# A two-layer decoder in one kernel: softmax probabilities turned by VectorE in squares of 32 and moved to their rows through DRAM

## The chip, the cores and the metric

The kernel runs on one core of a Trainium2 chip. A core has a matrix engine (TensorE), a vector engine (VectorE), a scalar engine (ScalarE), a general engine (GpSimd) and an engine that mainly issues transfers (SyncE, "SP" in the profile). Each has its own instruction stream; they meet through semaphores. The metric is the device time of one execution in microseconds (us): the median of the kernel before is 2106.39 us over three runs (2104.89 to 2107.31).

## What is computed

The input `x` is 16 sequences of 128 tokens with 512 features, all in 32-bit floats, and a context of 16 times 128 tokens with 128 features. Two decoder layers follow each other. In each, three sublayers are added to `x`, and each sum is normalized:

```
x = LN(x + attention(x));  x = LN(x + cross(x, ctx));  x = LN(x + ffn(x))
```

- Layer 0, attention: 16 heads of 32 features share 4 key and value heads. A mask of 1 on and below the diagonal is added to the scores, then softmax, values, an output projection with a bias.
- Layer 0, cross attention: 16 heads over the context, with key and query weights that the kernel first multiplies together ("folds").
- Layer 0, FFN: two ternary input weights, a gate, and a ternary output weight.
- Layer 1, attention: a linear attention with decay; it has no softmax.
- Layer 1, cross attention: 16 heads of 32 features, causal mask, scores divided by the root of 32, softmax, output projection.
- Layer 1, FFN: a shared expert, and eight experts of which each token uses two.

The change touches the first attention and the last cross attention. These have the same core, for each sequence and head:

```
p = softmax(q @ k.T * scale + mask)      # 128 queries x 128 keys
out = p @ v                              # then out @ wo.T over all heads
```

The scores come out with a query on each of the 128 partitions (rows of on-chip memory), since softmax sums along a row. TensorE sums over partitions, so for `p @ v` the keys have to be on the partitions: every `p` must be transposed, 16 matrices of 128x128 for each sequence.

## The kernel before

A block is one sequence (`P` = 128 tokens), of which there are `NB` = 16; a group is `GB` = 4 blocks, and there are `NG` = 4 groups. `x` stays on chip, one tile a block. PSUM, in which TensorE writes its results, has eight banks; `psum.share` (line 75) deals them out by tag: `mm` for projections and the transposes of `x`, `sc` for scores, `pt` for transposed probabilities and for the values' result. In both attentions it gives `mm` 2, `sc` 4, `pt` 2.

The sublayers run one after the other: the first attention at about 34 to 260 us of the profiled execution, the latent cross attention to 755, the ternary FFN to 1062, the linear attention to 1290, the last cross attention (the second one that the change touches; its first projections lie between 1290 and 1314) to 1522, routing and the shared expert to 1700, the experts to the end.

Both softmax attentions use one loop, `attend` (line 227). It is software pipelined over `n` from 0 to 17: `score(n)` issues the 16 small score matmuls of block `n` into four banks, one for each chunk of four heads. `value(n - 2)` multiplies the turned probabilities of the block two earlier with its values into a `pt` bank; ScalarE copies that to `oT` (line 246). Then come four steps, one for each chunk `c`:

- `Softmax.start`: VectorE adds the mask into a tile `t` (line 184) and takes the row maximum (line 186); ScalarE takes four exponentials with their row sums (line 191).
- `Softmax.finish`, for the chunk one earlier: VectorE takes the reciprocal of the sums (line 197) and GpSimd scales `p` (line 198).
- `Softmax.turn`, for chunk `c` of block `n - 1`: four TensorE transposes into a `pt` bank (line 203), and a VectorE copy to `pT` (line 205).
- at `c == 1` the output projection of block `n - 2`, `project_out` (line 144): four matmuls `po` (line 148), the residual add on VectorE (line 149), the statistics (line 110 on) and the normalization on GpSimd (line 121). At the other steps `share.deal()` issues a share of the next group's preparation.

The preparation (`prepare`) transposes four blocks of `x` on TensorE (lines 127 and 128), and projects queries, keys and values with 512-column matmuls (line 137, `chain`; tiles `pq`, `pk`, `pv`). In the first attention, preparation tasks of the later groups also hold the folding of the cross attention's weights (`fold`, line 274; its result `pg` in line 304). The weights to fold come as tiles `raw` of 1.7 MB each, two buffers, loaded by SP (line 391); a load waits for the fold two before it. After the last group, four of these folds and the rotation of the context (`dkv`, line 383) are what is left.

In the last cross attention each block's `x` is stored to a DRAM table `sums` as soon as it is normalized (line 987); the experts' results are added into that table later. Two tables in DRAM, `slots_x` (the tokens sorted by expert) and the tail of `sums`, must be zero before the experts start. The kernel writes these zeros (10 MB each) at the start of that cross attention's preparation (lines 897 to 899): GpSimd sets a tile `zero`, and two DMAs spread it.

A scheduler orders the instructions of each engine by the program and its own planned costs. SP issues nearly all transfers on one queue, in order: an issue that has to wait for a semaphore holds up all behind it.

The FFN between (`p3`, from line 672) runs over the four groups; its weights `w1`, `w2`, `w3` come in pieces of 352 KB through SP, and behind them the weights `wq4` of the linear attention. The latent cross attention turns its own probabilities otherwise: VectorE transposes within squares of 32 (line 590).

## Time and profile before

| | |
|---|---|
| median of three runs | 2106.39 us (2104.89 to 2107.31) |
| the profiled execution | 2109.23 us |
| its span on the core | 2107.5 us |
| busy: TensorE, weight loads | 2053.2 us (97%), 1148.5 us (54%) |
| busy: VectorE, ScalarE, GpSimd | 853.9 us (41%), 626.0 us (30%), 648.2 us (31%) |
| transposes of `p`, 128 x 4 on TensorE, copies on VectorE | 86.5 us of VectorE for the 128 copies (678 ns each) |
| scaling on GpSimd (three attentions) | 192 x 1048 ns = 201.1 us |
| exponentials of the masked attentions on ScalarE | 512 x 390 ns = 198.6 us |
| moved by DMA | 209.99 MB, 100 GB/s over the span |

The profiled execution's time is a little above the median, and its span is 1.7 us shorter than its time. Busy times are sums of instruction durations; those of TensorE overlap in the pipeline, so that the time a matmul adds is read from the distance of two starts, not from its duration. In lines that list instructions the tile written stands left of `<-`, the tiles read right of it, then shapes and the count. A clock of 1.00 is TensorE's full speed; the mean of this execution is 0.995. An entry such as "idle before, releaser" says how long an engine stood before the instructions of a group and what ended most of it.

### The profile page before, as it was taken

How to read it: one execution, taken by the hardware profiler on the slowest of the kernel's cores; microseconds unless marked ns; L12 is line 12 of the kernel's file. 1: busy time of each engine (PE TensorE's matmuls, PEld its weight loads, DVE VectorE, ACT ScalarE, POOL GpSimd, SP SyncE). 2: the span in 40 equal slices, each digit the busy share in tenths (PEclk: the TensorE clock that was granted, in tenths of full speed). 3: DMA queues.
4: the chain of work that ended last, by engine and by line, in shares of the span. 5: the costliest groups of instructions: out<-in, count | busy, mean ns of one | idle time of the engine just before them, and what ended most of it. 6: DMA issues, size and time to landing. Idle time of an engine off the chain costs nothing. (4 is left out here: it accounts for less than half of the span.)

```text
span 2107.5 us, 26857 instructions
## 1 busy us (share of the span) xinstructions
PE 2053.2 (97%) x10117; PEld 1148.5 (54%) x10117; DVE 853.9 (41%) x1728; ACT 626.0 (30%) x2167; POOL 648.2 (31%) x674
## 2 busy tenths in 40 slices
PE   8999999999999999999999999999899999999997
PEld 5555554445454458888555444555544455555552
DVE  4667733444554243222123313777731122222224
ACT  3655533323333222222211112766622200000002
POOL 5565521211122122223223113455603222222223
PEclk9999999999999999999999999999999999999999
DMA  6011320212220010001300008600004279999974
GB/s 230 1 35 45 112 79 24 62 43 74 60 66 6 1 54 2 1 1 39 115 1 1 1 6 258 232 21 21 27 25 147 93 244 284 303 294 293 289 229 166
DMA packets 105362, 209.99 MB, mean 100 GB/s; under 512 B 27280, under 2 KB 65552, under 8 KB 98576
## 3 DMA queue, kind: packets, MB, share of 16 engines
q1 hardware_dynamic: 90336, 101.40, 15.4%
q0 software_dynamic: 13792, 105.55, 15.2%
q8 instruction: 80, 1.31, 0.3%
q10 hardware_dynamic: 1104, 1.31, 0.2%
q14 instruction: 50, 0.41, 0.1%
HBM read 159.66 MB, written 48.57 MB: 99 GB/s over the span
## 5 line engine op out<-in xcount | busy, mean ns | idle before, releaser
L198 POOL TENSOR_TENSOR p<-p,rs 128x512 f32<-128x512 f32 x192 | 201.1, 1048 | 505.4 <-DVE rs L197 478.3
L613 PE MATMUL po<-mT,cc 128*128 128x512 f32 x512 | 236.0, 605 | 0.0
L191 ACT ACTIVATE p<-t,nmx 128x128 f32<-128x128 f32 x512 | 198.6, 390 | 34.5 <-POOL p L198 8.8
L613 PEld LDWEIGHTS po<-mT,cc 128*128 128x128 f32 x512 | 92.2, 189 | 107.2 <-issue 103.6
L191 ACT ACTIVATE p<-sc,nmx 128x128 f32<-128x128 f32 x256 | 90.2, 373 | 147.4 <-DVE nmx L186 142.1
L114 POOL TENSOR_SCALAR ve<-mv 128x1 f32<-128x1 f32 x80 | 18.1, 227 | 328.2 <-DVE mv L112 316.2
L559 PE MATMUL pq<-xT,wqr 128*128 128x512 f32 x256 | 117.5, 602 | 1.0 <-ACT xT L128 0.7
L1171 ACT ACTIVATE rsg<-rg 128x352 f32<-128x352 f32 x39 | 18.1, 464 | 336.0 <-PE rg L1166 336.0
L148 PE MATMUL po<-wo,oT 128*128 128x512 f32 x256 | 116.8, 599 | 0.4 <-ACT qkT L416 0.4
L1166 PE MATMUL rg<-ew,xsT 128*128 128x352 f32 x312 | 101.2, 466 | 14.5 <-DMA ew<-in_l1f_w_dram,which 12.7
L783 PE MATMUL pq<-xT,wq 128*128 128x512 f32 x256 | 110.9, 594 | 1.0 <-ACT xT L128 0.7
L1187 PE MATMUL ry<-ew,ractT 128*128 128x512 f32 (+1 forms) x234 | 106.9, 592 | 0.0
L121 POOL TENSOR_SCALAR x<-x,mv,rstd 128x512 f32<-128x512 f32 x48 | 100.6, 2097 | 4.5
L1166 PE MATMUL ru<-ew,xsT 128*128 128x352 f32 x312 | 98.7, 459 | 0.0
L191 ACT ACTIVATION_READ_ACCUMULATOR p<-t,nmx 128x1 f32 x512 | 96.4, 188 | 0.0
L706 POOL TENSOR_TENSOR hl<-ht,hh 128x512 fp32r<-128x512 f32 x44 | 60.5, 1375 | 114.8 <-ACT hh L704 114.8
L1137 POOL DMA_INDIRECT ew<-in_l1f_w_dram,which x39 | 38.1, 976 | 185.9 <-PE ry L1187 163.3
L1197 POOL DMA_INDIRECT sums<-ry,place x39 | 62.0, 1590 | 105.7 <-DMA sums<-ry,place 66.4
L205 DVE COPY pT<-pt 128x512 f32<-128x512 f32 x128 | 86.5, 678 | 18.1 <-PE pt L203 18.1
L203 PEld LDWEIGHTS pt<-ident,p 128*128 128x128 f32 x512 | 59.8, 141 | 53.8 <-issue 44.6
L1049 PE MATMUL pg<-xT,sw_gu 128*128 128x512 f32 x192 | 86.5, 593 | 0.0
L1173 DVE TENSOR_TENSOR ract<-rsg,ru 128x352 f32<-128x352 f32 x39 | 20.3, 521 | 158.5 <-issue 145.5
(231 smaller groups left out, 3715.4 us busy)
## 6 DMA issues: line engine op xcount, KB each, us to landing
piece<-in_l0f_w_dram SPq DMA_DIRECT2D x48, 352.0 KB
raw<-in_l0x_raw_dram SPq DMA_DIRECT2D x8, 1728.0 KB
slots_x<-zero SPq DMA_DIRECT2D x1, 10023.0 KB
sums<-zero SPq DMA_DIRECT2D x1, 9984.0 KB
xs<-slots_x SPq DMA_DIRECT2D x156, 64.0 KB
rep<-dkv SPq DMA_DIRECT2D x64, 64.0 KB
sums<-x SPq DMA_DIRECT2D x16, 256.0 KB
sum<-sums SPq DMA_DIRECT2D x16, 256.0 KB
```

Of the source, the lines that this page charges most:

```text
L121: engine.tensor_scalar(x[b], x[b], mean, rstd, ALU.subtract, ALU.mult)
L148: nc.tensor.matmul(po, lhsT=oT[:, c, :], rhs=wo[:, c, :], start=(c == 0), stop=(c == KC - 1))
L191: nc.scalar.activation(self.p[:, j, :], src[:, j, :], AF.Exp, bias=nmx[:, j : j + 1], accum_out=self.sm[:, j : j + 1])
L198: nc.gpsimd.tensor_tensor(self.p, self.p, spread(rs, P), ALU.mult)
L205: nc.vector.tensor_copy(self.pT, pt)
L559: nc.tensor.matmul(pq, lhsT=wqr[:, k, cols], rhs=xT[:, k, :], start=(k == 0), stop=(k == KC - 1))
L613: nc.tensor.matmul(self.po, lhsT=self.cc[:, 4 * par + j, :], rhs=mT[h], start=(par == 0 and j == 0), stop=(par == 1 and j == 3),)
L783: nc.tensor.matmul(pq, lhsT=wq4[k // 2][:, k % 2, c * P : (c + 1) * P], rhs=xT[:, k, :], start=(k == 0), stop=(k == KC - 1))
L1049: nc.tensor.matmul(dst, lhsT=sw_gu[:, k, at : at + P], rhs=xTs[g][:, k, :], start=(k == 0), stop=(k == KC - 1),)
L1166: nc.tensor.matmul(dst, lhsT=self.xT[:, k, :], rhs=gu[:, k, off : off + FE], start=(k == 0), stop=(k == KC - 1),)
L1187: nc.tensor.matmul(po, lhsT=self.actT[:mw, m_, :], rhs=dn[:mw, m_, :], start=(m_ == 0), stop=(m_ == 2))
L1197: nc.gpsimd.indirect_dma_start(out=sums, out_offset=bass.IndirectOffsetOnAxis(ap=place, axis=0), in_=y, in_offset=None, compute_op=ALU.add,)
```

## The change

The probabilities of the two attentions are no longer transposed by TensorE.

- `Softmax.start` adds the mask straight into the tile `p` (five buffers); the tile `t` is gone.
- A class `Turn` takes the place of `Softmax.turn`. `squares(c, p)` is one VectorE transpose for each chunk of four heads, which turns every 32x32 square in place and orders the result by key square. After each second chunk one SP store moves the pair (512 KB) to a DRAM tile `away` (two buffers). After the fourth, `back` reads it in four SP loads: load `k` brings the squares of keys 32`k` to 32`k`+31 to partitions 32`k` to 32`k`+31 of `pT`, a tile for all 16 heads with one buffer.
- In `attend`, `squares` of a chunk is called two chunk steps after its `start`; `value(n - 2)` and the copy to `oT` move from the head of the iteration to step 1, and the output projection to step 2.
- Both `value` functions read the new `pT`, in runs of 32 elements, and issue their matmuls in program order.
- In both attentions `psum.share` gives `mm` 3, `sc` 4, `pt` 1.
- The tables `slots_x` and `sums` and their clearing move to the FFN: issued in its second group (`g == 1`), in program order.

```diff
-    psum.share(mm=2, sc=4, pt=2)
+    psum.share(mm=3, sc=4, pt=1)
...
         def start(self):
+            if self.p is None:
+                self.p = self.pool.tile([P, 4, P], F32, tag="p", name="p", bufs=5)
             src = self.sc
             if self.mask is not None:
-                src = self.pool.tile([P, 4, P], F32, tag="t", name="t", bufs=3)
+                src = self.p
                 nc.vector.tensor_tensor(src, self.sc, bc(self.mask, 4), ALU.add)
...
-        def turn(self):
-            pt = bank("pt", [P, 4, P], "pt")
-            for j in range(4):
-                nc.tensor.transpose(pt[:, j, :], self.p[:, j, :], ident)
-            self.pT = self.pool.tile([P, 4, P], F32, tag="pT", name="pT", bufs=4)
-            nc.vector.tensor_copy(self.pT, pt)
+    class Turn:
...
+        def __init__(self, pool):
+            self.pool = pool
+            self.away = dram.tile([P, 4, 2, 8 * Q], F32, tag="away", name="away", bufs=2)
+
+        def squares(self, c, p):
+            if c % 2 == 0:
+                self.sq = self.pool.tile([P, 4, 8, Q], F32, tag="sq", name="sq", bufs=2)
+            at = slice(c % 2 * 4, c % 2 * 4 + 4)
+            nc.vector.transpose(
+                self.sq[:, :, at, :].rearrange("p k h q -> p h k q"), p.rearrange("p h (k a) -> p h k a", a=Q)
+            )
+            if c % 2:
+                nc.sync.dma_start(self.away[:, :, c // 2, :], self.sq.rearrange("p k h q -> p k (h q)"))
+            if c == 3:
+                self.back()
+
+        def back(self):
+            self.pT = self.pool.tile([P, 4, 16, Q], F32, tag="pT", name="pT", bufs=1)
+            rows = self.away.rearrange("(t a) k n f -> k a t (n f)", a=Q)
+            for k in range(4):
+                nc.sync.dma_start(self.pT[k * Q : (k + 1) * Q].rearrange("a t h q -> a t (h q)"), rows[k])
...
-            if n >= 2:
-                av = bank("pt", [P, KC, P], "av")
-                value(av, n - 2, [s.pT for s in held.pop(n - 2)])
-                oT = pool.tile([P, KC, P], F32, tag="oT", name="oT")
-                nc.scalar.copy(oT, av)
             for c in range(4):
                 if n < NB:
                     held[n][c].start()
                     late.append(held[n][c])
                 if late and (len(late) > 1 or n >= NB):
                     late.pop(0).finish()
-                if 1 <= n <= NB:
-                    held[n - 1][c].turn()
                 if c == 1 and n >= 2:
+                    av = bank("pt", [P, KC, P], "av")
+                    held.pop(n - 2)
+                    value(av, n - 2, turns.pop(n - 2).pT)
+                    oT = pool.tile([P, KC, P], F32, tag="oT", name="oT")
+                    nc.scalar.copy(oT, av)
+                of, part = divmod(4 * n + c - 2, 4)
+                if 0 <= of < NB:
+                    if part == 0:
+                        turns[of] = Turn(pool)
+                    turns[of].squares(part, held[of][part].p)
+                if c == 2 and n >= 2:
                     project_out(oT, wo, n - 2)
...
-                nc.tensor.matmul(av[rows], lhsT=v[:, n % GB, rows], rhs=pT[c], start=True, stop=True)
+                tc.keep_in_program_order(nc.tensor.matmul(
+                    av[rows], lhsT=v[:, n % GB, rows],
+                    rhs=pT[:, :, 4 * c : 4 * c + 4, :].rearrange("p t h q -> p h t q"), start=True, stop=True,
+                ))
...
+            if g == 1:
+                zero = p3.tile([P, D + 2], F32, tag="zero", name="zero")
+                nc.gpsimd.memset(zero, 0.0)
+                for t, rows, width in ((slots_x, NT, D + 2), (sums[NB * P :], NT, D)):
+                    tc.keep_in_program_order(nc.sync.dma_start(
+                        t.rearrange("(n p) d -> p n d", p=P), zero[:, 0:width].unsqueeze(1).broadcast_to([P, rows, width])
+                    ))
...
-        psum.share(mm=2, sc=4, pt=2)
+        psum.share(mm=3, sc=4, pt=1)
...
-                zero = p5.tile([P, D + 2], F32, tag="zero", name="zero")
-                nc.gpsimd.memset(zero, 0.0)
-                for t, rows, width in ((slots_x, NT, D + 2), (sums[NB * P :], NT, D)):
-                    nc.sync.dma_start(
-                        t.rearrange("(n p) d -> p n d", p=P), zero[:, 0:width].unsqueeze(1).broadcast_to([P, rows, width])
-                    )
...
-                    nc.tensor.matmul(
-                        av[j * HD : (j + 1) * HD, c, :], lhsT=v[:, h * HD : (h + 1) * HD], rhs=pT[j][:, c, :],
-                        start=True, stop=True,
-                    )
+                    tc.keep_in_program_order(nc.tensor.matmul(
+                        av[j * HD : (j + 1) * HD, c, :], lhsT=v[:, h * HD : (h + 1) * HD],
+                        rhs=pT[:, :, 4 * j + c, :], start=True, stop=True,
+                    ))
```

## The prediction

> **What bounds the kernel now.** I read first the busy time of each engine in stretches of the span (columns: stretch, its length, busy us and instructions of PE, PEld, DVE, ACT and POOL, granted clock, DMA share, GB/s). The two attentions that the change touches lie at about 34 to 260 us and 1314 to 1522 us.
>
> ```profile
> 40.00:240.00 200.00, 198.90 (x1303) 115.28 (x1304) 140.40 (x293) 122.98 (x529) 113.23 (x112) 0.98 0.12 42
> 1290.00:1530.00 240.00, 229.90 (x1717) 130.22 (x1718) 158.51 (x325) 145.70 (x592) 115.94 (x117) 1.00 0.29 106
> ```
>
> TensorE is the bound in both, with VectorE at about 70% and ScalarE at about 60%: time taken from TensorE can come out of the span until VectorE or a wait takes over. The second view is TensorE's timeline of one block of the first attention (start, length, records; two per matmul, one per transpose).
>
> ```profile
> 112.56 1.17 PE L446 MATMUL sc<-qkT 32*128 32x128 f32 x32
> 113.66 1.07 PE L452 MATMUL av<-pT,v 128*32 128x512 f32 x8
> 114.66 0.66 PE L203 MATMUL pt<-ident,p 128*128 128x128 f32 x4
> 115.15 2.74 PE L137 MATMUL pq<-xT,wr 128*128 128x512 f32 x6
> 117.73 0.60 PE L203 MATMUL pt<-ident,p 128*128 128x128 f32 x4
> 118.17 3.60 PE L148 MATMUL po<-wo,oT 128*128 128x512 f32 x8
> ```
>
> The starts give the prices: scores 1.10 us a block, values 1.00, output projection 3.43, four transposes 0.44 to 0.50. The 273 ns that the groups give for one transpose is latency, not cost. The starts also show the cover: between `av` and `po` stand 4.5 us of transposes and projections, in which ScalarE copies `av` to `oT`. Third come three waits and two durations:
>
> ```profile
> 1518.35 3.70 PE L148 MATMUL po<-wqo,oT 128*128 128x512 f32 x8 [0.73 <-ACT oT L246]
> L205 DVE COPY pT<-pt x128: 655/680/692, 50.2 to 1515.8; 128x512 f32<-128x512 f32 x128
> L590 DVE STREAM_TRANSPOSE pT<-p x64: 711/711/712, 289.4 to 743.2; 128x512 f32<-128x512 f32 x64
> POOL p L198: 74.7, 64
> SPq L391 <- PE pg L304: 139.7, 4, 107.4
> SPq L987 <- POOL x L121: 179.0, 16, 15.4
> ```
>
> The first is the last block, where nothing covers the copy: 0.73 us of idle TensorE. The fourth belongs to the 64 transposes of the cross attention, which VectorE already does: they waited 74.7 us for GpSimd's scaling, 1.17 us each. The last two say that SP's queue stood for 139.7 us in front of four `raw` loads until TensorE had freed their buffers, and 179.0 us in front of sixteen stores of `x` into `sums`. Nothing urgent is behind them now.
>
> **The change, part by part.** *Transposes.* 16 a block leave TensorE: 4 x 0.45 = 1.8 us, 28.8 us an attention, 57.6 in all. *The uncovered copy.* In the compiled order of the changed kernel `po` follows `av` at once in nearly every block, so it waits for `oT`: 0.8 us (the 0.73 above and a hop), 32 times, 25.6 us back. The net for TensorE is 1.0 us a block, 32 in all.
>
> *VectorE.* Copies of 680 ns become transposes of 711: 4 x 0.03 = 0.1 us a block. Worse is the order. VectorE used to leave scaled probabilities to TensorE; now it waits for GpSimd itself, and as the masked scores are written straight into `p` (five buffers), the fourth add of a block stands behind a transpose, and the transposes behind three reciprocals. I walk one cycle of the compiled order. Its work is four adds, four maxima and four transposes at 0.60 to 0.65, four reciprocals at 0.1, the residual add and statistics 1.4: 9.1 us, against 9.0 us from block to block in the tail of before. The third reciprocal must wait until ScalarE has done its chunk: two chunks of 1.55 us are pending when VectorE runs dry, 2.0 us of idle. The cycle is 11.1 us. Where ScalarE also has `qkT` copies (0.67 us) between, the loop residual add, next chunks, exp, `oT` 0.75, `po` 3.6, residual add comes to 12.3. TensorE's own blocks take 12 to 13.5 us while projections last, so this is mostly hidden there; it shows at the start and in the tail.
>
> *Start.* In the first attention blocks 0 and 1 now take four rounds each of reciprocal, scaling 1.04, transpose and hops, 1.85 us a round, 11.4 us a block. The first `av` comes at about 64 us (60.0 now, plus projections drawn ahead, 4.3, and scores, 1.7, less transposes, 1.8), its residual add at 70; 12 us later VectorE has emptied the scores that stand ahead of the second `av`: 82.4 for 74.5 now, 8 us late. The second attention starts 10 us late in the same way (its first residual add at 1352).
>
> *The way through DRAM.* A block writes 1 MB in two stores and reads it in four loads. Runs of 2 KB went at 352 GB/s in the clearing (6.68 MB in 19 us), a store and the load that waits for it lay 2.9 us apart for 256 KB, and four loads took 1.76 us to issue:
>
> ```profile
> 293.35 0.37 SPq L383 DMA_DIRECT2D dkv<-kvr  x1
> 296.61 1.76 SPq L538 DMA_DIRECT2D rep<-dkv  x4
> q1 hardware_dynamic: 3251, 6.68, 97.9%
> q1 hardware_dynamic: 1632, 0.79, 6.9%
> ```
>
> A 512 KB store takes 0.4 + 1.5 + 2 = 3.9 us; the four loads 1.7 to issue and about 2.7 after, 4.4 to 5. `pT` has one buffer, so loads start after the values of the block before, and have the 9 to 13 us of TensorE work between two `av`: covered, except in the last blocks of the second attention. Here a rule weighs against the change: each load fills 32 partitions, and by the Trainium skill (SBUF — State Buffer, on the DMA port swizzle) these reach 8 of 16 ports, 27.2 GB/s each, 218 GB/s: an estimate of 4.8 us for the 1 MB in place of 3.5. The row is the last one above: 1632 packets of `rep`, which fill 32 partitions too, took 6.9% of 16 engines' 40 us, 27 ns for 512 B, 303 GB/s. I take the row; by the rule about 1.3 us more for each of six uncovered blocks, 8 us.
>
> *SP's order.* In the compiled order two `raw` loads stand among the four loads of `pT` for blocks 11 and 12, and a third ahead of the stores for block 11. A `raw` load waits for the fold two before it, 8 to 9 us after the preceding `av`; the loads behind come after that and after 1.7 MB of transfer (4.7 us at the rates above): the `av` comes some 17 us after the one before, where TensorE's work is 10.2 and 9.4. Two stalls of 7 us, 14. In the second attention the stores of `x` (256 KB) stand ahead of the loads two blocks on, and wait for a layernorm which ends 11 us after `av`: about when these loads could start anyway; 0 in the middle.
>
> *Clock.* After small matmuls and transposes TensorE's clock fell to half for 7 us near 40 us:
>
> ```profile
> 38.00:40.00 2.00, 1.51 (x15) 1.15 (x14) 1.93 (x5) 2.00 (x13) 2.00 (x3) 0.94 0.03 14
> 42.00:44.00 2.00, 2.00 (x5) 0.97 (x4) 1.44 (x4) 2.00 (x12) 1.04 (x1) 0.50 0.00 0
> ```
>
> By the Trainium skill (TensorE: Matmul & The Clock Gate, Part 1) an idle window of 3.4 us throttles, and as long a busy one releases: 1.7 us lost for each 7 us stall. The row lost 7 us x 1/2 = 3.5 without such a gap. Two stalls give 3.4 or 7; I take 5.
>
> *Of no cost.* The clearing (a 0.53 us memset on GpSimd, two DMAs which keep SP 18.7 us and the engines 58 us) moves behind the last weight piece on SP, ahead of `wq` loads that wait for TensorE anyway; were that cover gone, 18.7 us late would still not reach the next stage. In its old place TensorE idled only 1.6 us from 1290 to 1350, so nothing is won either. One `pt` bank: `oT` frees it 10 us before the next `av`. The third `mm` bank can save the 0.3 us waits of the `x` transposes, at most 3 us; I take 0. The values now read runs of 32 elements, as the cross attention's do at no visible price: 0, at worst 1.0 us a block.
>
> **The sum**, against the profiled execution of before, 2109.23 us (span 2107.5, 1.7 around it). First attention: start +8; second to tenth block, eight at -1.0 less what VectorE takes back, -6; the last six, 14 of stalls less 9, by the work left on TensorE, +5; clock +5: +12. Second attention: start +10; second to eleventh block, nine from 13.4 to 12.5, -8; from there to its end 5.6 to the residual add, two cycles 22.4, squares 1.5, store 3.9, loads 5, values 1.2, copy and projection 4.2 = 43.8 for 49.5 now, -6: -4. In all +8, so 2117 profiled, and 2114 to 2115 beside the median of 2106.39.
>
> **Rivals.** (a) *TensorE stays the bound*: VectorE's waits and SP's order hide behind the projections, and only the net of 32 us counts: 2075. For it speaks VectorE's 70%; against it the 1.17 us waits above, which its busy share does not show. It decides if the cycle stays under about 11 us in all blocks and no `pT` load stands longer than 9 us. (b) *SP's order does not bite*, as TensorE is late enough when it gets to blocks 11 and 12: without 14 + 5 us of stall and clock, 2096. Against it: the waits of 139.7 us show how long such loads stand. (c) *The round trip becomes the bound*: at half the port rate and with stores queued ahead of the loads, a read lasts 9 to 10 us, and values follow each other in 11 to 12 even in blocks with little work, with more half-speed clock: +8 and 16 blocks at about 1.5 more: 2138.
>
> **How the numbers follow.** Likeliest 0.43, (a) 0.14, (b) 0.18, (c) 0.25. Faster by over 0.2% (about what a measurement tells from no change, 4.2 us): all of (a), two thirds of (b), a little of the likeliest: 0.29; within: 0.12; slower: 0.59. The range runs from near (a), 2084, to a little past (c), 2144; the likeliest's own is 2104 to 2126.
>
> **What would show it.** Right: no transposes at 0.44 us, `po` waiting 0.7 to 0.8 us for `oT` in most blocks, VectorE waiting for ScalarE at the reciprocal about 2 us a block, two gaps of about 7 us before `av` of blocks 11 and 12 that end with a `pT` load, the clock at half after them; the clearing under the FFN without a mark. Wrong: a VectorE cycle under 11 us and `av` never waiting for DMA (then (a)); or waits for `pT` loads in most blocks (then (c)).

## The result

The changed kernel takes 2178.05 us in the median (2171.53 to 2179.42) beside 2106.85 us (2104.89 to 2111.79) for the kernel before: the ratio is 1.0337, with a 95% interval of 1.0315 to 1.0358. That is 71 us slower. The forecast was 2115 us, slower by 8, and its range ended at 2144; the direction was right, the size not.

### The profile after

The span of the profiled execution is 2176.4 us, with a mean clock of 0.968 (0.995 before). First the busy time of each engine in the stretches that answer to those shown of before (stretch, its length, busy us and instructions of PE, PEld, DVE, ACT and POOL, granted clock, DMA share, GB/s). The second attention now starts 33 us later, so its stretch is moved.

```profile
40.00:240.00 200.00, 176.87 (x1005) 99.90 (x1003) 129.23 (x272) 114.90 (x506) 106.50 (x105) 0.91 0.59 163
1322.00:1562.00 240.00, 211.20 (x1266) 116.11 (x1264) 146.63 (x301) 133.43 (x563) 98.96 (x99) 0.88 0.47 131
```

TensorE was busy for 198.9 and 229.9 us of these lengths; now it is idle for 23 and 29 us and runs at a clock of 0.91 and 0.88. No other engine has become full: VectorE and ScalarE are less busy than before. The DMA share in the first attention has gone from 0.12 to 0.59. So nothing took TensorE's place as a full engine; the engines wait for each other.

TensorE's timeline of one block in the middle of the first attention:

```profile
119.19 1.06 PE L476 MATMUL av<-pT,v 128*32 128x512 f32 x8
121.01 3.70 PE L149 MATMUL po<-wo,oT 128*128 128x512 f32 x8 [0.76 <-ACT oT L273]
124.55 7.03 PE L138 MATMUL pq<-xT,wr 128*128 128x512 f32 x16
131.51 2.32 PE L470 MATMUL sc<-qkT 32*128 32x128 f32 x32
133.75 1.06 PE L476 MATMUL av<-pT,v 128*32 128x512 f32 x8
```

The transposes are gone, and `po` follows `av` with 0.76 us of idle, as forecast. But the scores, issued in one go in 1.1 us before, now take 1.65 to 2.3: the last of them wait for VectorE to free a bank. The block takes 14.6 us, as before.

The start of each block's values (blocks counted from 0), read from such timelines (second attention: counted from the stage's first transpose of the context), shows where the time went:

| block | first attention, before / after / later by | second, before / after / later by |
|---|---|---|
| 0 | 60.0 / 65.6 / 5.6 | 48.8 / 53.1 / 4.3 |
| 1 | 74.2 / 88.2 / 14.0 | 62.6 / 76.0 / 13.4 |
| 3 | 99.4 / 119.2 / 19.8 | 87.1 / 108.4 / 21.3 |
| 9; second: 7 | 186.8 / 204.0 / 17.2 | 142.1 / 176.7 / 34.6 |
| 12; second: 11 | 223.9 / 261.6 / 37.7 | 191.1 / 228.6 / 37.5 |
| end of the stage | 262.1 / 296.6 / 34.5 | 239.4 / 283.6 / 44.2 |

Three places lose: the first blocks of both attentions (20 us each), blocks 11 and 12 of the first (20 us), and the middle and end of the second (23 us). In between, the first attention wins some 3 us back twice; together 78.7 us. The stage of the experts is 8.1 us shorter (406.4 for 414.5); with its code unchanged it lay between 395.5 and 414.5 us in the profiled executions of this study, so no cause is looked for there. The lengths of the two attentions are the better measure, and the table below gives them beside the medians.

Blocks 11 and 12 of the first attention show the stall that was forecast. TensorE, then SP's queue at the same place (start, length, instruction):

```profile
230.00 6.35 PE L470 MATMUL sc<-qkT 32*128 32x128 f32 x32 [2.05 <-DVE p L187]
239.11 1.94 PE L476 MATMUL av<-pT,v 128*32 128x512 f32 x8 [2.76 <-DMA pT<-away]
...
261.57 1.94 PE L476 MATMUL av<-pT,v 128*32 128x512 f32 x8 [8.74 <-DMA pT<-away]
```

```profile
222.60 0.32 SPq L225 DMA_DIRECT2D pT<-away  x1
227.17 0.35 SPq L415 DMA_DIRECT2D raw<-in_l0x_raw_dram  x1
227.57 1.74 SPq L225 DMA_DIRECT2D pT<-away  x3
...
252.22 0.35 SPq L415 DMA_DIRECT2D raw<-in_l0x_raw_dram  x1
252.62 0.43 SPq L225 DMA_DIRECT2D pT<-away  x1
```

One load of `pT` goes at 222.60, the other three stand behind a `raw` load until 227.57; the values start at 239.11. In the next block the last load stands until 252.62, and the values at 261.57. The two blocks take 22.1 and 22.5 us where 10.8 and 11.0 stood.

The middle of the second attention is different. No wait for a load stands there; this is the chain of waits through one block:

```profile
1440.51 0.93 PE sc L966 x11
1441.44 1.27 DVE p L187 x2
1442.71 1.19 DVE nmx L189 x2
1443.90 0.61 DVE p L187
...
1445.34 2.79 ACT p L192 x14
...
1448.18 0.59 ACT oT L273
...
1448.82 6.65 PE po L149 x8
```

Scores of a later block are issued ahead of the values of this one; VectorE adds the mask and takes maxima, ScalarE does 14 exponentials, and only then comes the copy to `oT`, on which `po` waits. `po` takes 6.65 us in place of 3.6, since the clock is at half:

```profile
1442.00:1444.00 2.00, 1.53 (x12) 1.34 (x12) 2.00 (x5) 0.60 (x3) 0.00 (x0) 1.00 0.34 131
1444.00:1446.00 2.00, 1.45 (x6) 1.35 (x6) 1.27 (x3) 2.00 (x11) 0.61 (x1) 0.64 0.04 12
1446.00:1448.00 2.00, 2.00 (x33) 1.38 (x32) 0.18 (x1) 2.00 (x12) 1.47 (x2) 0.50 0.00 0
1450.00:1452.00 2.00, 2.00 (x4) 0.84 (x3) 1.92 (x4) 0.61 (x3) 0.00 (x0) 0.50 1.02 230
```

Over the whole execution four waits answer to the sum of the prediction (who waited, for whom: us in all, times, longest):

```profile
DVE rs L198 <- ACT p L192: 82.2, 72, 2.2
PE po L149 <- ACT oT L273: 32.8, 30, 2.7
SPq L1014 <- POOL x L122: 115.8, 15, 9.8
SPq L415 <- PE pg L328: 22.5, 4, 9.9
```

The transposes on VectorE, from the list of the costliest groups (busy us, mean ns of one, then the idle time before):

```profile
L213 DVE STREAM_TRANSPOSE sq<-p 128x512 f32<-128x512 f32 x128 | 86.7, 693 | 31.2 <-POOL p L199 18.5
```

### The profile page after: what moved, and what is told of

It is laid out like the page before. It is cut to its first block, busy times and chain, and to the rows that moved or that the text cites. A ratio compares the mean times of both kernels' runs of the same rounds, so it can differ in the third digit from the quotient of the medians.

```text
span 2176.4 us, 25991 instructions
## 1 busy us (share of the span) xinstructions
PE 2061.9 (95%) x9605; PEld 1143.2 (53%) x9605; DVE 852.8 (39%) x1728; ACT 624.3 (29%) x2167; POOL 647.4 (30%) x674
## 3 DMA queue, kind: packets, MB, share of 16 engines
q0 software_dynamic: 13792, 105.55, 14.6%
## 4 chain that ended last, share of the span: by engine, by line
PE 84%; DMA 6%; DVE 3%; ACT 3%; POOL 2%; issue 1%; SPq 0%; ACTq 0%; POOLq 0%; DVEq 0%
PE po L639 11%; PE po L149 9%; PE pq L585 5%; PE pq L821 5%; PE pq L138 4%; PE pg L1076 4%; PE ry L1214 4%; PE pa L733 4%; PE pb L733 4%; PE po L760 4%; PE rg L1193 4%; DMA ew<-in_l1f_w_dram,which 4%; PE ru L1193 3%; PE pu L1076 3%; PE av L626 3%; PE po L138 3%
## 5 line engine op out<-in xcount | busy, mean ns | idle before, releaser
L192 ACT ACTIVATE p<-p,nmx 128x128 f32<-128x128 f32 x512 | 198.6, 391 | 107.1 <-DVE nmx L189 77.0
L149 PE MATMUL po<-wo,oT 128*128 128x512 f32 x256 | 127.7, 646 | 15.4 <-ACT oT L273 15.4
L213 DVE STREAM_TRANSPOSE sq<-p 128x512 f32<-128x512 f32 x128 | 86.7, 693 | 31.2 <-POOL p L199 18.5
L192 ACT ACTIVATION_READ_ACCUMULATOR p<-p,nmx 128x1 f32 x512 | 96.8, 189 | 0.0
L149 PEld LDWEIGHTS po<-wo,oT 128*128 128x128 f32 x256 | 49.8, 204 | 86.5 <-issue 54.4
L149 PE MATMUL po<-wqo,oT 128*128 128x512 f32 x128 | 77.8, 764 | 17.6 <-ACT oT L273 17.5
```

The costliest lines, as they stand in the source:

```text
L149: nc.tensor.matmul(po, lhsT=oT[:, c, :], rhs=wo[:, c, :], start=(c == 0), stop=(c == KC - 1))
L192: nc.scalar.activation(self.p[:, j, :], src[:, j, :], AF.Exp, bias=nmx[:, j : j + 1], accum_out=self.sm[:, j : j + 1])
```

## The experiments

Each kernel is the changed one with one edit, unless said otherwise. "Over" is the difference of its median to that of the kernel before, measured beside it (the changed kernel: 71); the last columns are the lengths of the two attentions in its profiled execution, the first counted from the execution's start. These lengths come from one execution each. Where an edit leaves an attention alone, they still differ by up to 4 us (the first attention: 295.9 in pT2b, 292.6 in sums_pool, 296.6 in the changed kernel), so smaller differences are not read. no_dram, raw_once, the wide kernels and the two without `raw` compute another output: they measure a cost and are no candidates.

| kernel | over, us | ratio, 95% interval | first | second |
|---|---|---|---|---|
| before | | | 262.1 | 239.4 |
| changed | 71 | 1.0337 [1.0315, 1.0358] | 296.6 | 283.6 |
| clear_only | 0 | 0.9997 [0.9984, 1.0010] | 262.4 | 239.4 |
| late_add | 71 | 1.0338 [1.0310, 1.0366] | 296.5 | 281.5 |
| cover | 62 | 1.0309 [1.0284, 1.0335] | 297.2 | 276.2 |
| no_dram | -4 | 0.9981 [0.9971, 0.9992] | 262.7 | 241.7 |
| raw_once | 52 | 1.0250 [1.0217, 1.0283] | 274.0 | 280.0 |
| shallow | 58 | 1.0274 [1.0242, 1.0306] | 294.8 | 271.1 |
| pT2b | 72 | 1.0340 [1.0295, 1.0384] | 295.9 | 282.9 |
| sums_pool | 59 | 1.0287 [1.0253, 1.0321] | 292.6 | 274.7 |
| best | 63 | 1.0308 [1.0283, 1.0333] | 296.0 | 270.8 |
| best_wide | 32 | 1.0158 [1.0124, 1.0191] | 283.8 | 253.0 |
| warm | 97 | 1.0449 [1.0426, 1.0472] | 309.6 | 284.2 |
| mm2 | 76 | 1.0363 [1.0342, 1.0385] | 295.3 | 289.8 |
| wide_loads | 12 | 1.0060 [1.0041, 1.0079] | 273.1 | 249.2 |
| best_noraw | 45 | 1.0215 [1.0189, 1.0241] | 287.4 | 268.6 |
| best_wide_noraw | 13 | 1.0064 [1.0038, 1.0090] | 271.3 | 252.0 |
| mix16 | 87 | 1.0408 [1.0391, 1.0425] | 300.1 | 292.2 |
| two_q | 87 | 1.0414 [1.0397, 1.0432] | 304.4 | 288.4 |
| wide_deep | 28 | 1.0133 [1.0116, 1.0150] | 282.1 | 253.4 |

### Which part costs: the clearing, VectorE's place, the copy, or the way through DRAM

The first theory after the result came from VectorE's waits: in the sixteen blocks of the second attention it stood 45.8 us for `po`, at the residual add, with the mask adds of later blocks behind (17.6 us of it in the last two blocks; the 3.2 us a block in the forecast below also took in waits of the stage before). The rival was the way through DRAM.

**clear_only.** The kernel before, with the tables and their clearing moved as in the change:

```diff
+            if g == 1:
+                zero = p3.tile([P, D + 2], F32, tag="zero", name="zero")
+                nc.gpsimd.memset(zero, 0.0)
...
-                zero = p5.tile([P, D + 2], F32, tag="zero", name="zero")
```

> The kernel before with one part of the change: the tables slots_x and sums and their clearing move into the FFN; both attentions stay as before. If the clearing costs nothing there and the tables' place is indifferent: 2107 us within 4. If the 8 us by which the expert phase of the changed kernel is shorter (414.5 us from its first gate matmul to the end before, 406.4 after) come from the clearing's new place: 2098 to 2100.

Measured: no difference, and both attentions as long as before within 0.4 us. The clearing costs and brings nothing. The 8 us of the expert stage did not follow it.

**late_add.** `project_out` only issues `po`; the residual add and the statistics come two steps of the loop later, pinned behind the maximum of the third chunk there:

```diff
+        later.append((po, b))
+        return
...
                     held[n][c].start()
+                if c == 2 and n >= 4:
+                    add_out(later)
```

> The changed kernel, with only the residual add and statistics of a block moved on VectorE: behind the mask adds and maxima of three chunks of the block after, in place of ahead of them. Loop theory (VectorE stands for the output projection, so the scores of later blocks get no bank, TensorE runs dry and falls to half clock): the waits of the residual add, 3.2 us a block in the last cross attention, go; 20 to 40 us less than the changed kernel, 2138 to 2158. Theory of the way through DRAM (the loads of pT set the distance of two blocks): no change, 2174 to 2182.

Measured: the time of the changed kernel. The residual adds wait 17.8 us in place of 45.8, nearly all in the last two blocks, and the middle is as slow (119.2 us from block 3 to block 11, for 120.3). The theory falls: VectorE's wait at the residual add was, in the middle, idle time that cost nothing. The chain above shows why: it runs through the mask adds, exponentials and `oT`, not through that add.

**cover.** The work dealt at step 1 goes behind the values, `po` behind that work:

```diff
-                else:
+                elif c == 1 and n >= 2:
+                    with tc.issue_after(got.ins):
+                        share.deal()
+                else:
                     share.deal()
```

> The changed kernel, with the preparation work of one step put between the values and the output projection on TensorE, as it stood before, so that ScalarE's copy of the values' result is hidden. If the uncovered copy only costs its own wait (33 us in all, of which 20 us are in blocks that have preparation work): 2155 to 2165. If its gaps are also what drops the clock: 2135 to 2150. If VectorE's loop sets the distance of the blocks anyway: 2172 to 2180.

Measured: 9 us less than the changed kernel, 7 of them in the second attention. The waits of `po` for `oT` fall from 33 to 9 us in all, but the first attention is no shorter: what is won there is waited for at the next place, as its scores wait 17.0 us for VectorE to free a bank, in place of 8.6.

**no_dram.** Stores and loads are left out:

```diff
-                nc.sync.dma_start(self.away[:, :, c // 2, :], self.sq.rearrange("p k h q -> p k (h q)"))
-            if c == 3:
-                self.back()
+                self.sqs.append(self.sq)
...
-                    rhs=pT[:, :, 4 * c : 4 * c + 4, :].rearrange("p t h q -> p h t q"), start=True, stop=True,
+                    rhs=pT[c // 2][:, :, c % 2 * 4 : c % 2 * 4 + 4, :].rearrange("p k h q -> p h k q"), start=True, stop=True,
```

> The changed kernel without the way through DRAM: the stores and loads are left out, and the values read the squares where VectorE wrote them, so the output is another. The work of TensorE, VectorE, ScalarE and GpSimd stays; the planner now also puts projections between the values and the output projection. Loop theory: the 26 us of waits that end with a load of pT go, and some half clock behind them, but VectorE's loop stays: 2125 to 2150. Theory of the way through DRAM: the attentions come to what TensorE needs, 2075 to 2095.

Measured: 4 us below the kernel before, the attentions 3 us longer together. All of the loss comes by the way through DRAM: its own time, or the order that is made around it. It also shows what there was to win: little. With the turned probabilities for nothing, TensorE's stretches look like this:

```profile
40.00:240.00 200.00, 184.38 (x1081) 96.07 (x1080) 141.37 (x293) 119.69 (x527) 113.38 (x112) 0.95 0.13 48
1290.00:1530.00 240.00, 217.51 (x1446) 110.66 (x1445) 158.50 (x324) 141.67 (x590) 115.65 (x116) 0.93 0.05 20
```

TensorE's busy time falls by 14.5 and 12.4 us against before, but the stretches do not get shorter: it is idle instead, and part of the time at half clock. The 32 us that the prediction called the net of the change are not there even with free transfers.

### The stalls one by one

**raw_once.** Of six `raw` loads in the first attention four are left out:

```diff
-                raw = rawp_.tile([P, 2, RAW], F32, tag="raw", name=f"raw{i}")
-                nc.sync.dma_start(raw, a["l0x_raw"][i].rearrange("p (h n) -> p h n", h=2))
+                if i < 2:
+                    raws[i] = rawp_.tile([P, 2, RAW], F32, tag="raw", name=f"raw{i}")
+                    nc.sync.dma_start(raws[i], a["l0x_raw"][i].rearrange("p (h n) -> p h n", h=2))
+                raw = raws[i % 2]
```

> The changed kernel, with four raw loads of the first attention left out: folds 2 to 5 work on the weights of folds 0 and 1, which lie on chip already, so the output is another. TensorE's work and nearly all of the order stay. SP's order (the loads of pT for blocks 11 and 12 stand behind raw loads): the two blocks at 22 us from values to values come to 11, and with them goes the half clock behind; 18 to 24 us less than the changed kernel, 2154 to 2160. If the loads of pT are late of themselves there: 2172 to 2180.

Measured: 20 us less than the changed kernel; its first attention is 22.6 us shorter. The values of blocks 11 to 13 in its timeline:

```profile
229.28 1.06 PE L480 MATMUL av<-pT,v 128*32 128x512 f32 x8
240.17 1.06 PE L480 MATMUL av<-pT,v 128*32 128x512 f32 x8
249.07 1.07 PE L480 MATMUL av<-pT,v 128*32 128x512 f32 x8 [0.32 <-PE pm L321]
```

10.9 and 8.9 us from block to block, and no wait for a load. The stall of blocks 11 and 12 comes by the `raw` loads, as forecast, and its price is known. This run takes away both SP's wait and the transfer of 1.7 MB, so it does not say which of them costs.

**shallow.** In the compiled order of before, `48 + 16 b` score matmuls stand ahead of the values of block `b`; in the changed kernel it is up to `76 + 16 b`, in the first attention for all of blocks 1 to 11: 1.75 blocks more. This kernel pins the scores behind the values of three blocks earlier, and the exponentials behind the copy to `oT`:

```diff
+                with ExitStack() as behind:
+                    if n >= 3:
+                        behind.enter_context(tc.issue_after(got.ins))
+                    score(sc, n)
...
+                    with ExitStack() as behind:
+                        if n >= 3:
+                            behind.enter_context(tc.issue_after(copied.ins))
+                        held[n][c].start()
```

> The changed kernel, with the order around the values as before: TensorE issues the values of block b ahead of the scores of block b + 3, where the changed kernel's compiled order has scores up to three quarters of block b + 4 ahead of them; ScalarE copies them to oT ahead of all but two chunks of exponentials of block b + 2, where the changed order has 20 more of the single exponentials ahead. All work and the way through DRAM stay. If the planner's order is what costs (deeper pipeline at the start, oT behind exponentials in the middle): 2135 to 2155, with the start of both attentions 10 to 18 us earlier. If the loads of pT themselves need the long lead: 2175 to 2200, with values that wait for pT in most blocks.

Measured: 13 us less, below the 23 to 43 expected; the second attention is 12.5 us shorter. Its blocks 3 to 7 now take 13.8 us each, as before. Its start is still 11 us late, and its blocks 10 to 14 wait 2.7 to 6.6 us each for a load: with less lead the lateness of the loads is seen. Both theories were half right.

**pT2b, sums_pool.** A second buffer for `pT` in the second attention (`bufs=2`, with `xT` at one), and the stores of `x` into `sums` issued by GpSimd (`nc.gpsimd.dma_start` for `nc.sync.dma_start`).

> The changed kernel with two buffers of pT in the last cross attention (the room comes from the second buffer of xT there). The order of the instructions stays but for some on ScalarE. If the single buffer is what makes the last four blocks take 43 us: 7 to 14 us less, 2164 to 2171. If the loads there stand behind the stores of x into sums, or the middle of this attention is bound elsewhere: 2174 to 2182.

> The changed kernel with the sixteen stores of x into sums issued by GpSimd, which has just normalized x, in place of SP. If these stores hold up the loads of pT behind them (SP stood 115.8 us for them in all, of which the loads can have used the part in the last six blocks): 4 to 15 us less, 2163 to 2174. If they only fill time in which the loads could not start: 2176 to 2182.

Measured: nothing for the buffer, 12 us less for the stores, 9 of them in the second attention, whose last blocks wait 1.8 and 3.0 us for loads in place of 6.4 and 6.3. A load that stands behind a store on the queue isn't helped by a free buffer.

**best.** shallow, cover and sums_pool together, and the `raw` loads of the first attention issued by ScalarE:

```diff
-                nc.sync.dma_start(raw, a["l0x_raw"][i].rearrange("p (h n) -> p h n", h=2))
+                nc.scalar.dma_start(raw, a["l0x_raw"][i].rearrange("p (h n) -> p h n", h=2))
```

> The changed kernel with four corrections together, all work kept: values ahead of later scores as in shallow; projections between values and output projection as in cover; raw loads of the first attention issued by ScalarE; stores of x into sums by GpSimd. If the four effects measured alone add up (raw 20, sums 12, order 14, cover 10): 2122. If they share the same half clock: 2125 to 2140. If the way through DRAM costs nothing once nothing stands in its way: 2098 to 2106, as without it.

Measured: 63 over, no better than each alone. The gains don't add up. In both attentions most blocks now wait for a load of `pT` (11 and 10 of 16), 24 us in each. So part of the visible stalls were only places where late loads came to the surface.

### The loads themselves

The loads were put at 303 GB/s in the prediction. Here is the traffic while a block's loads run in the changed kernel (1 us steps; clock, DMA share and GB/s stand last; a share of 1 means that all 16 DMA engines are busy):

```profile
181.00:182.00 1.00, 1.00 (x4) 0.42 (x3) 1.00 (x3) 0.97 (x6) 0.00 (x0) 1.00 1.05 231
182.00:183.00 1.00, 1.00 (x4) 0.52 (x3) 1.00 (x3) 0.29 (x1) 0.00 (x0) 1.00 1.11 215
183.00:184.00 1.00, 1.00 (x3) 0.39 (x3) 1.00 (x4) 1.00 (x7) 0.56 (x1) 1.00 1.01 212
```

The engines are full at 212 to 231 GB/s. Single steps of other blocks lie lower and higher (315 and 205 GB/s from 235 to 237 us). Each load fills only 32 partitions. In the program, **wide_loads** and **best_wide** change that alone, in the changed kernel and in best; the bytes, the runs of 2 KB and the places read in DRAM stay:

```diff
-            rows = self.away.rearrange("(t a) k n f -> k a t (n f)", a=Q)
+            rows = self.away.rearrange("p k n f -> k p (n f)")
             for k in range(4):
-                nc.sync.dma_start(self.pT[k * Q : (k + 1) * Q].rearrange("a t h q -> a t (h q)"), rows[k])
+                nc.sync.dma_start(self.pT[:, k].rearrange("p h q -> p (h q)"), rows[k])
```

> As best, but each of the four loads of pT fills all 128 partitions with a quarter of the columns, in place of 32 partitions with all columns; bytes, run length (2 KB) and the number of loads stay, the squares come to other places, so the output is another. If 32 partitions hold the transfer down (the loads of the changed kernel ran at 208 to 224 GB/s while all 16 engines were busy, stores at 350): loads near 350 GB/s, and 4 to 20 us less than best. If the port makes no difference: the same rate, and best's time within 4 us.

> The changed kernel with one thing other: each of the four loads of pT fills all 128 partitions with a quarter of the columns, in place of 32 partitions with all; bytes, runs and the number of loads stay, the squares come to other places, so the output is another. The planner answers with an order like that of before (values of block b ahead of the scores of block b + 3). If the slow narrow loads are the root, through their rate and through the order planned around them: 30 to 45 us over the kernel before (the changed kernel is 71 over, best_wide 32). If raw loads, the stores of x and the oT order on ScalarE weigh as much as they did in the changed kernel: 50 to 70 over.

Measured: best_wide is 32 over where best is 63, and wide_loads only 12 over: this one property, with the order that is compiled around it, gives back 59 of the 71 us, more than was expected. With fast loads the corrections of best no longer help but cost 20 us; no run tells which of them. The same view of wide_loads:

```profile
131.00:132.00 1.00, 1.00 (x3) 0.38 (x2) 1.00 (x2) 1.00 (x6) 0.00 (x0) 1.00 1.03 352
132.00:133.00 1.00, 1.00 (x4) 0.52 (x3) 0.28 (x2) 1.00 (x7) 0.55 (x1) 1.00 0.94 354
```

And a block in the middle of its second attention, with scores, values and `po` in the order of before, projections over the copy, and 13.3 us from `po` to `po` (1404.58 to 1417.87):

```profile
1409.93 1.17 PE L966 MATMUL sc<-kT,qT 32*128 32x128 f32 x32
1411.03 1.98 PE L138 MATMUL pq<-xT,wqo 128*128 128x512 f32 x4
1412.95 1.08 PE L973 MATMUL av<-pT,v 128*32 128x128 f32 x32
1413.96 1.12 PE L138 MATMUL pq<-xT,wqo 128*128 128x512 f32 x2
...
1417.87 3.70 PE L149 MATMUL po<-wqo,oT 128*128 128x512 f32 x8 [0.66 <-ACT qT L951]
```

wide_loads changes two things at once, since its compiled order has `48 + 16 b` scores ahead of the values again. **wide_deep** makes it deeper by one block, by taking the values one step later:

```diff
-        for n in range(NB + 2):
+        for n in range(NB + 3):
...
-                if c == 1 and n >= 2:
+                if c == 1 and n >= 3:
...
-                    value(av, n - 2, turns.pop(n - 2).pT)
+                    value(av, n - 3, turns.pop(n - 3).pT)
```

> wide_loads, but the program takes the values of a block one step later (block n - 3 in step n), so that the scores run one block further ahead: four fifths of a block short of the order in the changed kernel; the output is another, as in wide_loads. wide_loads is 12 us over the kernel before. If a deeper pipeline costs its filling in both attentions: 25 to 42 over. If the depth costs nothing as long as loads are fast: 6 to 16 over.

Measured: 28 over, 16 more than wide_loads, 13.2 in the attentions' lengths. Depth costs, even with fast loads. So there are two ways from wide_loads (522.3 us of attention) to the changed kernel (580.2): slow loads first, order after (shallow 565.9: 43.6, then 14.3), or one block of depth first (wide_deep 535.5: 13.2, then 44.7 for slow loads and the rest of the order). They come out alike: about 44 us by the rate of the loads, about 14 by the order. The split is rough, since the orders of shallow and wide_loads also differ elsewhere. The 18 us from no_dram (504.4) to wide_loads are the trip with fast loads. In wide_loads the values of blocks 0 to 11 come no more than 3 us later than before in either attention, and mostly earlier; what it loses, it loses behind them. In the second attention four of the last five blocks wait for a load, 12.1 us in all.

**best_noraw, best_wide_noraw.** The edit of raw_once in both:

> best without four raw loads of the first attention (folds 2 to 5 work on the weights of folds 0 and 1, so the output is another). best is 62 us over the kernel before. If raw transfers in front of loads of pT still cost there, though another queue issues them: 42 to 52 over. If the narrow loads alone set the distance: 58 to 64 over.

> best_wide without the same four raw loads; output is another. best_wide is 32 us over the kernel before, with its last blocks of the first attention at 15 to 18 us each, some 20 us late. If raw transfers are what makes them late: 10 to 18 over. If the round trip (store, load, a wait of 8 us from issue to values) sets the tail by itself: 26 to 34 over. Without any way through DRAM it was 4 below.

Measured: 17 and 19 us less over the kernel before than best and best_wide. The first attentions, where the edit is, are 8.6 and 12.5 us shorter, beside 22.6 in raw_once. In best and best_wide ScalarE issues the `raw` loads, so SP does not stand behind them: that these loads still cost there fits 1.7 MB in front of the loads of `pT` on the same engines. It is not shown alone, since ScalarE then waits for the folds itself.

**mix16, two_q.** Two attempts at fast loads that still put every square in its place: sixteen loads of 64 KB a block, in the order of partition groups 0, 2, 1, 3, and loads of the two halves on two queues:

```diff
-            for k in range(4):
-                nc.sync.dma_start(self.pT[k * Q : (k + 1) * Q].rearrange("a t h q -> a t (h q)"), rows[k])
+            for t in range(4):
+                for k in (0, 2, 1, 3):
+                    nc.sync.dma_start(self.pT[k * Q : (k + 1) * Q, t].rearrange("a h q -> a (h q)"), rows[k][:, t])
```

```diff
             for k in range(4):
-                nc.sync.dma_start(self.pT[k * Q : (k + 1) * Q].rearrange("a t h q -> a t (h q)"), rows[k])
+                queue = nc.sync if k < 2 else nc.scalar
+                queue.dma_start(self.pT[k * Q : (k + 1) * Q].rearrange("a t h q -> a t (h q)"), rows[k])
```

> The changed kernel with each of the four loads of pT cut into four, one for each square row, in the order of partition groups 0, 2, 1, 3: sixteen loads of 64 KB a block, the same bytes and runs, the output is right. The compiled order of all engines stays but for a few rows; SP issues for some 7 us a block in place of 1.7. If transfers to different groups of 32 partitions then run side by side, with the order kept: 8 to 25 us less than the changed kernel, 2153 to 2170, the loads at 260 GB/s or more. If the engines still go through one group at a time: 2178 to 2195, by the longer issue.

> The changed kernel with the loads of pT for the lower 64 partitions on SP's queue and those for the upper 64 on ScalarE's, so that two groups of partitions are filled at once; the output is right. ScalarE then waits itself for the stores and for pT to come free. The planner's order lies between that of before and that of the changed kernel. If the rate of the loads is the root and ScalarE can bear the waits: 20 to 45 over the kernel before. If ScalarE's waits hold up exponentials and copies: 60 to 90 over.

Measured: both are slower than the changed kernel. mix16 couldn't tell what it was made for: SP takes 7.3 us for the sixteen issues, 64 KB in each 0.46 us or 140 GB/s, and the traffic beside it is 133 to 152 GB/s with the engines half idle. two_q's traffic from 3 to 6 us after the loads of a block were issued on both queues at 165.1 us (a store was issued behind them at 167.2):

```profile
168.00:169.00 1.00, 1.00 (x6) 0.92 (x5) 1.00 (x3) 1.00 (x7) 0.00 (x0) 0.50 1.10 266
169.00:170.00 1.00, 1.00 (x11) 1.00 (x11) 1.00 (x2) 1.00 (x7) 0.00 (x0) 0.50 1.04 227
170.00:171.00 1.00, 1.00 (x9) 0.81 (x5) 0.25 (x2) 1.00 (x6) 0.67 (x1) 0.50 1.06 243
```

The engines are full at 227 to 266 GB/s: somewhat more than 212 to 231, and far from 352. The beginning of the store may be in the last of these. That two_q is slower all the same is put down to ScalarE's own waits for stores and buffers; no run separates them.

### The clock

**warm, mm2.** Two matmuls of 512 columns a block whose result isn't used, in a bank taken from `mm`; and the changed kernel with `mm` at two for comparison:

```diff
-    psum.share(mm=3, sc=4, pt=1)
+    psum.share(mm=2, sc=4, pt=1, warm=1)
...
                 score(sc, n)
+                keep_warm(1, wo)
...
                     nc.scalar.copy(oT, av)
+                    keep_warm(1, wo)
```

> The changed kernel with two matmuls of 512 columns a block added on TensorE in both attentions, into a bank taken from mm, one behind the scores, one behind the values: 64 x 0.86 = 55 us of added work whose result is not used. If the half clock lengthens the attentions (TensorE at half speed for a quarter of their time) and short gaps bring it about: the clock rises from 0.87 to 0.93 or more there and the time stays within 10 us of the changed kernel or falls, 2160 to 2188. If the half clock only fills time that is lost anyway: 2195 to 2235.

> The changed kernel with mm at two banks as before, the eighth bank unused: the comparison for warm. The third bank was put at 0 to 3 us: 2176 to 2182. If it carries more in the changed order: 2183 to 2195.

Measured: warm is 20 us slower than mm2, for 55 us of added work; half of the 20 lies in the expert stage, which the edit does not touch. The clock in the second attention is 0.94 (0.87 in the changed kernel), and that attention, with 27 us more to do, is 5.6 us shorter than in mm2 (284.2 for 289.8), while the first is 14 us longer. So half clock is a part of the loss in the second attention, of a few us net, and not the main one: no_dram ran at 0.95 and 0.93 and was no slower than the kernel before. The third bank is worth about 5 us at most: the intervals of mm2 and the changed kernel overlap.

## Why the prediction was wrong

**The loads' rate** is the step that failed, and most of the rest follows from it. The prediction weighed a row (303 GB/s, from 1632 packets of `rep`) against the rule in the Trainium skill (SBUF — State Buffer, the DMA port swizzle: 32 partitions reach 8 of 16 ports, 218 GB/s), took the row, and left the rule's 1.3 us more for each of six uncovered blocks, 8 us, out of the sum. Measured are 212 to 231 GB/s with full engines, in agreement with the rule's number, and 352 to 354 with all partitions; and the difference is 59 us, some 44 of it by the rate alone. The row was also misread. Its 40 us hold two more transfers beside `rep`, and only a third of its bytes are those of the four narrow loads; while these ran, the engines were busy for 0.22 to 0.45 of the time:

```profile
ct<-in_ctx_dram SPq DMA_DIRECT2D x1, 256.0 KB
dkv<-kvr SPq DMA_DIRECT2D x1, 256.0 KB
rep<-dkv SPq DMA_DIRECT2D x4, 64.0 KB
297.00:298.00 1.00, 1.00 (x12) 1.00 (x11) 0.64 (x2) 1.00 (x7) 0.00 (x0) 1.00 0.22 65
298.00:299.00 1.00, 1.00 (x14) 0.92 (x17) 0.36 (x1) 1.00 (x7) 0.00 (x0) 1.00 0.45 132
```

So it could not have shown the limit: four loads of 64 KB took 1.76 us to issue, which asks for 149 GB/s at most, and 132 went. A packet's time, taken while the engines are half idle, did not give the rate when they are full. That the ports are what limits is not shown here, and two_q does not test it: loads to both halves at once ran at 227 to 266 GB/s, and the same page (on two DMAs to hit both halves) says that such transfers serialize, with 6% gained.

**"Covered, except in the last blocks"** was the second error. It looked at whether a load of 5 us fits between two `av`, and it does: only 6 of 32 blocks wait for one. But a slow transfer also shares the engines with stores and `raw` loads, and the compiled order was deeper with it, by 1.75 blocks. The prediction read that order for `po` and for SP, and didn't count how many scores stand ahead of the values. With fast loads and the order of before, the phrase comes out right: wide_loads loses in the last blocks alone. That it then lies 12 us over, near the sum's 8, is luck; the sum had 18 us in the starts, where wide_loads loses nothing.

**Start** (+8 and +10): block 0 came 5.6 and 4.3 us late, near the sum's 4, but the next blocks added to it: block 1 was 14.0 us late where the sum had 8, block 3 was 20 and 21. The working took blocks 0 and 1 and stopped; filling 1.75 blocks more was a missing term. That depth costs by itself is shown by wide_deep, but shallow, with the scores no further ahead than before and slow loads, is still 12.6 and 11.6 us late at block 3: the depth is not all of it.

**Middle of the first attention** (-1.0 us a block): block 3 to block 9 took 84.8 us for 87.4, -0.4 a block. Of 1.8 us of transposes 0.76 to 1.5 went to the uncovered copy, as forecast (32.8 us measured for 25.6), and 0.6 to scores that wait for a bank, which the sum lacked.

**Middle of the second** (-8): block 3 to block 11 took 120.3 us for 104.0, +16. The loop of residual add, mask adds, exponentials, `oT` and `po` was put at 12.3 us and called hidden. It is the chain shown above, without the residual add (late_add); blocks took 11.2 to 16.0 us at full clock and up to 21.4 with half clock. With the scores no further ahead than before (shallow) the same stretch takes 107.5 us.

**End of the second** (-6): from block 11 on 54.9 us for 48.3. The stores of `x` ahead of the loads were put at 0 in the middle, which held, but they also delay the last loads: in sums_pool this end takes 47.7 us.

**SP's order** (14, and 5 for the clock) was right in place and near in size: two stalls at blocks 11 and 12, 22.8 us measured in these blocks, 20 to 23 with raw_once. **VectorE's wait** for ScalarE at the reciprocal was right in size: 63 us in the two attentions, 2.0 us a block. It is 4.9 us in all in no_dram, so it comes with the changed order and not with the work. What it costs by itself is not shown. (The work of its cycle was summed short: with the four transposes at the 711 ns named just before, it is about 9.6 us for the 9.1.) **Clearing, `pt` bank, runs of 32** at nothing: right for the clearing (clear_only), and `av` takes 1.06 to 1.08 us a block at full clock. The single `pt` bank was not tested alone; no_dram, which has it too, loses 3 us in both attentions. The `mm` bank at 0 is worth at most about 5.

**The rivals.** (a), TensorE stays the bound and 32 us are won, is refuted where it should hold best: without the way through DRAM 4 us are won. (b), SP's order doesn't bite, is refuted by the trace. (c), the round trip becomes the bound by half the port rate, had the right cause, but not the way it acts: its sign, waits for `pT` loads in most blocks, is seen in best and not in the changed kernel (6 of 32 blocks). Its 2138 was too low because it counted only the waits for loads and not what goes wrong ahead of them.

## What to carry to other kernels

A bandwidth is read from a row only if that row asks for the bandwidth: see whose packets the row counts, compare bytes by issue time with the rate before trusting the packets' time, and if a rule gives less for the shape in question, cost the change by the rule. A transfer that is covered in the steady state still costs where a pipeline fills, where a queue is shared and where the order is made around it, so count from the compiled order how much work stands ahead of its consumer. When several stalls each give back 10 to 20 us and together no more, look for one thing that makes them all late.

## What was not expected of the hardware

- Loads of the same bytes and runs of 2 KB: 212 to 231 GB/s into 32 partitions, 352 to 354 into 128, with the DMA engines full in both. What holds the narrow ones down stays open.
- TensorE's clock went to half without an idle stretch of 3.4 us: at 1444 to 1446 us the gaps were 0.58 and 0.85 us, in 4 us of scores in 32 rows. The Trainium skill (TensorE: Matmul & The Clock Gate, Part 1) speaks of an idle window of that length; here the clock fell without one. Whether the short gaps or the small matmuls brought it about, no run separates.
- With 27 us of useless matmuls the second attention was 5.6 us shorter (warm against mm2).
- VectorE's transpose of squares takes 693 ns for 128x512, close to the 711 ns of the cross attention, also with its output spread in pieces of 32.
